# Attention output of a graph-attention layer: 48 mixed matmuls per batch become 64 matmuls of one shape, in another order

## The chip, the cores and the metric

The kernel runs on one NeuronCore of a Trainium2 chip, in one launch. The metric is device time in microseconds (us), measured over whole executions; the kernel before takes 548.71 us (median of 3 runs, 548.39 to 549.91). The engines are named as in the profile: PE is TensorE's matmul side, PEld its weight loads, DVE is VectorE, ACT is ScalarE, POOL is GpSimd, SP issues DMAs.

## The reference

For each of 16 batches there are 512 nodes with 512 features. A dense layer gives `self_feat`; in each of two directions d every node attends, with 16 heads, over the first 20 nodes only. Cut to what matters here:

```python
kv = self_feat[:, :20]
aff = einsum('bnhd,bmhd->bnhm', qh, kh) / sqrt(32)
aff = where(cond > 0, aff, NEG) + label_bias          # per node and key
w = softmax(aff, axis=-1)                             # 512 nodes x 16 heads x 20 keys
out_t = einsum('bnhm,bmf->bnhf', w, kv)
out = einsum('bnhf,hgf->bnhg', out_t, Wout) + bout    # 32 outputs g per head
output = self_feat + out(d=0) + out(d=1)
result = v + relu(output)
```

All of it is in 32-bit floats. The kernel folds `Wout` into the values beforehand, so that per batch the last product is: weights (512 nodes x 640, that is 16 heads x 2 directions x 20 keys) times a block-diagonal value matrix (640 keys x 512 outputs).

## The kernel before, in words

A setup part (up to about 90 us) computes key, bias and value matrices for all batches and writes them to DRAM. Then a loop runs over the batches. Its order is written out by hand: under a manual schedule every engine gets its instructions in the order of the program text. The body for batch b mixes, on PE, the seven score products of batch b (a Strassen-like scheme of seven products in place of eight; helper `score_terms`, line 397, tiles `ps_a`, `ps_c`, `ps_d`), the seven products of the dense layer of batch b+1 (`self_product`, line 667, tile `ps_f`), and near its end the attention output of batch b-1 (`attend`, line 569, tiles `ps_o_f`, `ps_o_c`, and `ps_o_s` at the end of the program). The softmax of a block runs on DVE and ACT (`weigh`, `expo`, `total`), its scaling on POOL (`normal`), and `turn` (line 545) transposes it on DVE in 32x32 blocks into the tile `wt`. The last batch is written out after the loop, with `attend` called for pieces of the nodes.

In `attend`, the weights lie in `wt` with 32 keys on 32 partitions, four such blocks of rows (a = 0 to 3, one per quarter of the nodes), and in the free dimension the key half c (0 or 1), and inside it node groups and five blocks j of 32 keys. The values `vd` lie on the same 32 rows, eight blocks `at` of 32 outputs per key half. Block `at` uses the keys of block j, and it is added to the 32 output partitions `at // 2` of bank a. So `at` = 0, 1 go to output block 0, 2, 3 to block 1, 4, 5 to block 2 and 6, 7 to block 3. `at` 0, 3, 4, 7 are called outer here, 1, 2, 5, 6 inner; 1 and 2 share j = 1, and 5 and 6 share j = 3, so each of these pairs can be one matmul with 64 output columns on two neighbouring output blocks. All matmuls of `attend` add to what `seed_out` (line 556, on ACT) has put into the four PSUM banks before, and `finish` (line 586, on DVE) reads them a loop body later.

A matmul of `attend` uses 32 rows of the PE array (rows of block a) and 32 or 64 columns. Sixteen blocks of 32 by 32 fill the array; so do eight of 32 by 64.

Of the kernel before, what the change touches and what calls it, by code (L numbers as in the profile page):

```python
# [18 lines left out]
def gat_kernel(  # L19
# [21 lines left out]
    B, F, N = xT.shape  # L41
    NG, L = adj.shape[3], adj.shape[4]
    H, DH = 16, 32
# [8 lines left out]
    R = P // HL  # L52
# [41 lines left out]
    ksums, fsums, terms, weighs, smalls, cqD, nzD, outsum, outt, whole = [{} for _ in range(10)]  # L94
# [465 lines left out]
    def attend(b, spans=((0, 0, 2 * HL), (1, 0, 2 * HL)), banks=range(HL)):  # L560


        vd = vds[b].rearrange("p c e i g -> p c (e i g)")
        pairs, ones = ((1, 2, 1), (5, 2, 3)), ((0, 1, 0), (3, 1, 2), (4, 1, 2), (7, 1, 4))
        runs = (ones, spans[:1]), (pairs, spans), (ones, spans[1:])
        for c, lo, hi, at, n, j in [(*span, *of) for group, those in runs for span in those for of in group]:
            for a in banks:
                r = bass.ts(a, R)
                nc.tensor.matmul(  # L569
                    outsum[b][a][bass.ds(at // 2 * DH, n * DH), bass.ds(c * N // 2 + lo * R, (hi - lo) * R)].rearrange(  # L570
                        "p (n r) -> p n r", r=R
                    ),
                    vd[r, c, bass.ds(at * DH, n * DH)],
                    wts[b][r, c].rearrange("p l (g w) -> p (l g) w", g=HL)[:, lo:hi, bass.ts(j, 32)],
                    start=False, stop=n == 1 + (c == 0), skip_group_check=True,
                )

    def spread_out(t, a):
# [120 lines left out]
    with tc.tile_pool(name="setup", bufs=1) as sp, tc.tile_pool(name="ps_acc", bufs=4, space=PSUM) as acc["pool"]:  # L699
# [11 lines left out]
        ones = sp.tile([P, P], F32, name="ones")  # L711
# [6 lines left out]
        with tc.tile_pool(name="setup_k", bufs=1) as sk:  # L718
# [124 lines left out]
            of = {(d, 0): early[:, d] for d in range(2)}  # L843
# [16 lines left out]
        with tc.tile_pool(name="setup_g", bufs=3) as sg:  # L860
# [123 lines left out]
            while units:  # L984
                runs = []
# [84 lines left out]
    with tc.manual_schedule():  # L1070
# [4 lines left out]
        for b in range(B - 1):  # L1075
# [183 lines left out]
            if one:  # L1259
                attend(b - 1)  # L1260
                at(further, feat_sum, b + 1, 2)
                normal(b, 1, 0)
# [19 lines left out]
        b = B - 1  # L1282
# [34 lines left out]
        seed_out(o, 3)  # L1317
        seed_block(b, 1, 1, [accs.tile([P, 2, N // 2], F32, tag=f"f{i}", name=f"ps_e{i}") for i in range(2)])
        attend(o)
        turn(b, 0, 0)  # L1320
        total(b, 1, 0)
# [27 lines left out]
        weigh_plain(b, 1, 1, 1)  # L1349
        turn_part(b, 1, 1, 0)  # L1350
        attend(b, ((0, 0, 8),))
        attend(b, ((1, 0, 4),), range(2))
        spare = const.tile([P, C, WD], F32, tag="g", name=f"o{b}", bufs=1).rearrange("p c w -> p (c w)")
# [66 lines left out]
```

## Time and profile before

| what | value |
|---|---|
| time of whole executions | 548.71 us (548.39 to 549.91) |
| span of the profiled execution | 547.1 us |
| what lies around the span (difference to the median) | 1.6 us |
| PE busy, share of the span | 541.1 us, 99% |
| DVE busy | 481.1 us, 88% |
| POOL, ACT busy | 434 us, 404 us |
| one loop body in the steady part | 28.65 us |
| one `attend` of a whole batch | 2.39 us |
| granted TensorE clock, mean | 0.998 |

How it is read: the span runs from the first to the last instruction of one execution. "Busy" of PE is the union of its matmul records; matmuls are pipelined and the ends of their records are modelled, so what counts below is where records start. Each 32-bit matmul of the program stands in the trace as two passes, each with a weight-load record and a matmul record. The timeline merges neighbouring records of one group into one row with a count (x2); its first column is the start of the first of them in us from the span's start.

### The profile page before, as it was taken

How to read it: one execution, taken by the hardware profiler on the slowest of the kernel's cores; microseconds unless marked ns; L12 is line 12 of the kernel's file. 1: busy time of each engine (PE TensorE's matmuls, PEld its weight loads, DVE VectorE, ACT ScalarE, POOL GpSimd, SP SyncE). 2: the span in 40 equal slices, each digit the busy share in tenths (PEclk: the TensorE clock that was granted, in tenths of full speed). 3: DMA queues.
4: the chain of work that ended last, by engine and by line, in shares of the span. 5: the costliest groups of instructions: out<-in, count | busy, mean ns of one | idle time of the engine just before them, and what ended most of it. 6: DMA issues, size and time to landing. Idle time of an engine off the chain costs nothing.

```text
span 547.1 us, 19673 instructions
## 1 busy us (share of the span) xinstructions
PE 541.1 (99%) x7932; PEld 424.5 (78%) x7932; DVE 481.1 (88%) x711; ACT 404.2 (74%) x999; POOL 433.7 (79%) x418
## 2 busy tenths in 40 slices
PE   9999999999999999999999999999999999999996
PEld 6554368889888878787888888887878788878784
DVE  1776678889999999999999999999999999999996
ACT  1225436798887979888888888887878787978564
POOL 2637996779979797979798888888897979797664
PEclk9999999999999999999999999999999999999999
DMA  8999999978886878788776857676777676736034
GB/s 297 377 394 374 296 367 349 301 228 263 229 257 184 237 218 222 227 221 235 206 232 182 245 182 227 201 231 193 226 209 214 199 227 185 243 91 202 2 116 156
DMA packets 100546, 126.45 MB, mean 231 GB/s; under 512 B 19608, under 2 KB 68694, under 8 KB 98408
## 3 DMA queue, kind: packets, MB, share of 16 engines
q1 hardware_dynamic: 98856, 122.19, 71.7%
q0 software_dynamic: 1168, 2.23, 1.7%
q8 instruction: 62, 1.02, 0.7%
q10 hardware_dynamic: 432, 0.79, 0.4%
q14 instruction: 28, 0.23, 0.2%
HBM read 86.23 MB, written 40.24 MB: 231 GB/s over the span
## 4 chain that ended last, share of the span: by engine, by line
PE 97%; DVE 2%; ACT 0%; issue 0%; DVEq 0%
PE ps_f L667 32%; PE ps_a L397 24%; PE ps_c L397 11%; PE ps_d L397 6%; PE ps_o_f L569 5%; PE ps_v L893 3%; PE ps_k L831 3%; PE ps_kv L781 2%; PE ps_a L284 1%; PE ps_o_c L569 1%; PE ps_l L397 1%; PE ps_c L284 1%; PE ps_warm L737 1%; PE ps_o_s L569 0%; DVE o L611 0%; DVE w L465 0%
## 5 line engine op out<-in xcount | busy, mean ns | idle before, releaser
L327 ACT ACTIVATE prod<-adj,wb_sb 128x80 f32<-128x80 int32 x330 | 116.0, 429 | 0.0
L537 POOL TENSOR_TENSOR w<-w,sm 128x640 f32<-128x640 f32 x63 | 80.2, 1273 | 33.1 <-DVE sm L533 29.5
L667 PE MATMUL ps_f<-t,ws_s 128*64 128x246 f32 x720 | 80.0, 370 | 0.0
L667 PEld LDWEIGHTS ps_f<-t,ws_s 128*64 128x64 f32 x720 | 51.7, 137 | 18.9
L528 ACT ACTIVATE w<-w 128x640 f32<-128x640 f32 x60 | 43.8, 731 | 17.8 <-DVE w L524 17.8
L545 DVE STREAM_TRANSPOSE wt<-w 128x640 f32<-128x640 f32 x63 | 52.4, 833 | 0.1
L667 PE MATMUL ps_f<-x,ws_v 128*64 128x246 f32 x480 | 52.4, 371 | 0.0
L532 DVE TENSOR_REDUCE sm<-w 128x32 f32<-128x640 f32 x63 | 51.1, 811 | 1.1 <-ACT w L528 0.9
L523 DVE TENSOR_REDUCE ps_d<-w 128x32 f32<-128x640 f32 x59 | 48.7, 826 | 1.8 <-ACT ps_d L431 0.2
L524 DVE TENSOR_TENSOR w<-w,ps_d 128x640 f32<-128x640 f32 x59 | 48.4, 820 | 2.0
L667 PEld LDWEIGHTS ps_f<-x,ws_v 128*64 128x64 f32 x480 | 34.7, 137 | 13.0
L370 POOL TENSOR_TENSOR k<-g,k 128x608 f32<-128x608 f32 x30 | 44.7, 1489 | 0.0
L397 PEld LDWEIGHTS ps_a<-g,sf 128*64 128x64 f32 x544 | 34.3, 137 | 5.9 <-issue 5.8
L397 PE MATMUL ps_a<-g,sf 128*64 128x152 f32 x544 | 38.6, 295 | 0.0
L397 PE MATMUL ps_d<-g,sf 128*64 128x152 f32 x544 | 37.9, 293 | 0.0
L338 DVE TENSOR_REDUCE add<-prod 128x80 f32<-128x960 f32 x32 | 36.7, 1146 | 1.1 <-POOL prod L333 1.1
L346 ACT COPY both<-add 64x80 f32<-64x80 f32 x128 | 32.6, 255 | 5.7 <-DVE add L338 4.6
L569 PE MATMUL ps_o_c<-wt,vd 32*32 32x256 f32 (+1 forms) x720 | 36.8, 386 | 0.0
L682 POOL TENSOR_TENSOR t<-x,t 128x492 f32<-128x492 f32 x30 | 34.8, 1161 | 1.2
L397 PEld LDWEIGHTS ps_d<-g,sf 128*64 128x64 f32 x544 | 35.3, 137 | 0.2 <-ACT sf L685 0.2
L333 POOL TENSOR_SCALAR prod<-cond 128x80 f32<-128x80 f32 x32 | 18.0, 563 | 21.8 <-DVE cond L332 20.3
L569 PE MATMUL ps_o_f<-wt,vd 32*32 32x256 f32 (+1 forms) x672 | 34.5, 386 | 0.0
(300 smaller groups left out, 1435.9 us busy)
## 6 DMA issues: line engine op xcount, KB each, us to landing
g<-g_d SPq DMA_DIRECT2D x60, 304.0 KB
g_d<-st SPq DMA_DIRECT2D x16, 1064.0 KB
out_T<-o SPq DMA_DIRECT2D x64, 256.0 KB
x<-in_xT SPq DMA_DIRECT2D x56, 256.0 KB
xn<-in_xn SPq DMA_DIRECT2D x48, 256.0 KB
adj<-in_adj SPq DMA_DIRECT2D x52, 220.0 KB
vd<-bd_d SPq DMA_DIRECT2D x64, 64.0 KB
nz<-nz_d SPq DMA_DIRECT2D x14, 256.0 KB
```

The lines of the kernel that those rows point to most:

```text
L327: nc.scalar.activation(p[:, :, l], a[:, :, l], AF.Identity, scale=wb_sb[:, l : l + 1])
L338: done["masks"] = nc.vector.tensor_reduce(add, prods.pop((b, h)), AX.X, ALU.add)
L370: done["ksum"] = engine.tensor_sub(to, one, two)
L397: nc.tensor.matmul(slot(g)[bass.ts(p, P // 2), : HL * S].rearrange("p (h m) -> p h m", m=NG)[:, :, 1:], of(k)[:, bass.ds(first + g * P // ...
L523: nc.vector.tensor_reduce(mx, f, AX.X, ALU.max)
L524: done["weigh"] = (engine or nc.vector).tensor_sub(f, f, mx.unsqueeze(2).to_broadcast([P, per, NG]))
L528: done["exp"] = nc.scalar.activation(t, t, AF.Exp)
L532: nc.vector.tensor_reduce(sm, heads(weighs[b, c, l]), AX.X, ALU.add)
L537: done["normal"] = nc.gpsimd.tensor_mul(f, f, smalls.pop((b, c, l)).unsqueeze(2).to_broadcast([P, per, NG]))
L545: done["turn"] = nc.vector.transpose(wts[b][:, c, l], weighs.pop((b, c, l)).rearrange("p g w -> p (g w)"))
L569: nc.tensor.matmul(outsum[b][a][bass.ds(at // 2 * DH, n * DH), bass.ds(c * N // 2 + lo * R, (hi - lo) * R)].rearrange("p (n r) -> p n r", ...
L667: nc.tensor.matmul(parts[b][n in (2, 3, 5)][bass.ts(a, P // 2), bass.ts(i, HN)], lhs, x[:, k], start=False, stop=k == 1, skip_group_check= ...
```

## The change

`attend` no longer joins the inner pairs. All matmuls take 32 rows and 32 outputs, and the order is: the outer blocks of key half 0, the outer blocks of key half 1, the inner blocks of key half 0, the inner blocks of key half 1. Before it was: the outer blocks of half 0 (16 matmuls of 32x32), the joined inner pairs of both halves (16 matmuls of 32x64), the outer blocks of half 1 (16 of 32x32). The flag that ends a group is set on the inner blocks. The products and sums are the same. A call for a piece of the nodes goes through the same order with one key half.

```diff
         vd = vds[b].rearrange("p c e i g -> p c (e i g)")
-        pairs, ones = ((1, 2, 1), (5, 2, 3)), ((0, 1, 0), (3, 1, 2), (4, 1, 2), (7, 1, 4))
-        runs = (ones, spans[:1]), (pairs, spans), (ones, spans[1:])
-        for c, lo, hi, at, n, j in [(*span, *of) for group, those in runs for span in those for of in group]:
+        outer, inner = ((0, 0), (3, 2), (4, 2), (7, 4)), ((1, 1), (2, 1), (5, 3), (6, 3))
+        for c, lo, hi, at, j in [(*span, *of) for group in (outer, inner) for span in spans for of in group]:
             for a in banks:
                 r = bass.ts(a, R)
                 nc.tensor.matmul(
-                    outsum[b][a][bass.ds(at // 2 * DH, n * DH), bass.ds(c * N // 2 + lo * R, (hi - lo) * R)].rearrange(
+                    outsum[b][a][bass.ts(at // 2, DH), bass.ds(c * N // 2 + lo * R, (hi - lo) * R)].rearrange(
                         "p (n r) -> p n r", r=R
                     ),
-                    vd[r, c, bass.ds(at * DH, n * DH)],
+                    vd[r, c, bass.ts(at, DH)],
                     wts[b][r, c].rearrange("p l (g w) -> p (l g) w", g=HL)[:, lo:hi, bass.ts(j, 32)],
-                    start=False, stop=n == 1 + (c == 0), skip_group_check=True,
+                    start=False, stop=at in (1, 2, 5, 6), skip_group_check=True,
                 )
```

On PE, in the `attend` of a batch in the steady part, the place where the first 16 matmuls end and the joined pairs begin, before (a row is one matmul, x2 two; 32x256 is 32 outputs by 256 nodes; numbers behind names count buffers):

```order
L569 MATMUL ps_o_f_4208<-wt_3669,vd_4016 32x256
L569 MATMUL ps_o_f_4209<-wt_3669,vd_4016 32x256
L569 MATMUL ps_o_c<-wt_3669,vd_4016 32x256 x2
L569 MATMUL ps_o_f_4208<-wt_3669,vd_4016 64x256
L569 MATMUL ps_o_f_4209<-wt_3669,vd_4016 64x256
L569 MATMUL ps_o_c<-wt_3669,vd_4016 64x256 x2
```

In the changed kernel every row of `attend` is of 32x256, sixteen times these three rows, up to the score products that follow:

```order
L568 MATMUL ps_o_f_4304<-wt_3749,vd_4112 32x256
L568 MATMUL ps_o_f_4305<-wt_3749,vd_4112 32x256
L568 MATMUL ps_o_c<-wt_3749,vd_4112 32x256 x2
L397 MATMUL ps_a_4424<-g_4031,sf_4095 64x8x19 x16
L397 MATMUL ps_d_4426<-g_4031,sf_4095 64x8x19 x16
```

The shape no longer changes inside `attend`, 16 matmuls came in, and what stands before and behind it on PE is the same.

The second place is the end of the program on PE, the pieces of the last batch. Before:

```order
L569 MATMUL ps_o_s_7384<-wt_7357,vd_7251 32x128 x8
L569 MATMUL ps_o_s_7384<-wt_7357,vd_7251 64x128 x4
L569 MATMUL ps_o_s_7398<-wt_7357,vd_7251 32x192 x8
L569 MATMUL ps_o_s_7398<-wt_7357,vd_7251 64x192 x4
L569 MATMUL ps_o_s_7384<-wt_7357,vd_7251 32x64 x8
L569 MATMUL ps_o_s_7384<-wt_7357,vd_7251 64x64 x4
```

And now:

```order
L568 MATMUL ps_o_s_7624<-wt_7597,vd_7475 32x256 x2
L568 MATMUL ps_o_s_7638<-wt_7597,vd_7475 32x256 x2
L568 MATMUL ps_o_s_7624<-wt_7597,vd_7475 32x128 x16
L568 MATMUL ps_o_s_7638<-wt_7597,vd_7475 32x192 x16
L568 MATMUL ps_o_s_7624<-wt_7597,vd_7475 32x64 x18
```

Each piece is one run of equal matmuls in place of two runs of different shape. On the other engines nothing moves.

## The prediction

> **What bounds the kernel now.** I read the page first, then busy times by stretch, then PE's timeline inside one `attend`, since the diff touches nothing else. From the page:
>
> ```profile
> span 547.1 us, 19673 instructions
> PE 541.1 (99%) x7932; PEld 424.5 (78%) x7932; DVE 481.1 (88%) x711; ACT 404.2 (74%) x999; POOL 433.7 (79%) x418
> PEclk9999999999999999999999999999999999999999
> PE 97%; DVE 2%; ACT 0%; issue 0%; DVEq 0%
> q8 instruction: 62, 1.02, 0.7%
> ```
>
> The chain that ended last is PE for 97% of the span, at full clock. Busy times by stretch, cut at the first matmul of two `attend`s and at the first one behind each (columns: stretch, length, busy and records of PE, PEld, DVE, ACT, POOL, clock, DMA share, GB/s):
>
> ```profile
> 286.72:289.12 2.40, 2.40 (x99) 1.19 (x97) 2.28 (x3) 1.34 (x4) 2.32 (x3) 1.00 0.45 127
> 289.12:315.37 26.25, 26.25 (x347) 22.43 (x337) 24.68 (x36) 22.91 (x59) 21.95 (x21) 1.00 0.74 220
> 315.37:317.76 2.39, 2.39 (x98) 1.18 (x96) 2.27 (x3) 1.34 (x4) 2.31 (x3) 1.00 0.39 114
> 317.76:344.01 26.25, 26.25 (x347) 22.43 (x336) 24.69 (x36) 22.93 (x59) 21.94 (x21) 1.00 0.74 219
> ```
>
> PE has no idle time; a body of the loop is 26.25 + 2.39 = 28.65 us, the same each time. So a change of `attend`'s 2.39 us goes into the time one for one, as often as it runs in such a stretch. How often, from the list of the line's instructions (name, records, shortest/median/longest in ns, first and last start):
>
> ```profile
> L569 PE MATMUL ps_o_f<-wt,vd x672: 373/375/425, 143.3 to 518.0; 32*32 32x256 f32 x112, 32*64 32x256 f32 x56
> ```
>
> Two of four banks, 12 matmuls each, two passes each: 48 records per `attend`, so 672 are 14 of them, all in the stretch that PE bounds. The fifteenth (530.84) and the pieces of batch 15 lie in the tail, below.
>
> **The change part by part.** Inside one `attend` (PE's timeline; each row two records, `ps_o_f` banks 0 and 1, `ps_o_c` banks 2 and 3):
>
> ```profile
> 315.37 0.41 PE L569 MATMUL ps_o_f<-wt,vd 32*32 32x256 f32 x2
> 315.38 0.41 PE L569 MATMUL ps_o_c<-wt,vd 32*32 32x256 f32 x2
> 315.39 0.40 PE L569 MATMUL ps_o_f<-wt,vd 32*32 32x256 f32 x2
> ...
> 315.61 0.38 PE L569 MATMUL ps_o_f<-wt,vd 32*32 32x256 f32 x2
> ...
> 315.70 0.38 PE L569 MATMUL ps_o_c<-wt,vd 32*32 32x256 f32 x2
> 316.01 0.43 PE L569 MATMUL ps_o_f<-wt,vd 32*64 32x256 f32 x2
> 316.03 0.44 PE L569 MATMUL ps_o_c<-wt,vd 32*64 32x256 f32 x2
> 316.07 0.44 PE L569 MATMUL ps_o_f<-wt,vd 32*64 32x256 f32 x2
> 316.10 0.44 PE L569 MATMUL ps_o_c<-wt,vd 32*64 32x256 f32 x2
> 316.28 0.38 PE L569 MATMUL ps_o_f<-wt,vd 32*64 32x256 f32 x2
> ...
> 316.50 0.38 PE L569 MATMUL ps_o_f<-wt,vd 32*64 32x256 f32 x2
> ...
> 316.71 0.38 PE L569 MATMUL ps_o_f<-wt,vd 32*64 32x256 f32 x2
> ...
> 317.12 0.41 PE L569 MATMUL ps_o_f<-wt,vd 32*32 32x256 f32 x2
> 317.13 0.41 PE L569 MATMUL ps_o_c<-wt,vd 32*32 32x256 f32 x2
> 317.14 0.40 PE L569 MATMUL ps_o_f<-wt,vd 32*32 32x256 f32 x2
> ```
>
> Three groups, A (outer, half 0), B (pairs), C (outer, half 1): 0.64 + 1.11 + 0.64 us. In A the first passes of all 16 matmuls start within 0.1 us (eight rows, 0.013 apart, 6.7 ns per matmul), and the second passes from 315.61 on: a block of the array takes its second pass when its first has streamed, and other blocks' matmuls run past it meanwhile. B has eight blocks, so four rounds.
>
> *What is removed: two changes of shape.* Inside B a round follows the last by 0.215 us (316.28, 316.50, 316.71). The last round before another shape takes 0.40 (315.61 to 316.01, 316.71 to 317.12), the first one 0.24 to 0.27. The change keeps eight rounds (64 matmuls, 16 at a time, two passes) and one shape: if rounds simply followed each other, 0.24 + 6 x 0.215 + 0.40 = 1.93 us, 0.46 less than now.
>
> [...]
>
> *What is added: groups that follow each other without a pause, each of 16 x 4 = 64 instructions* (two weight loads and two matmuls per matmul). Whether PE has them at hand in time is not shown for one shape, but A to B shows how supply works. B's first matmuls start at 316.01, but the rows then come 0.033 apart, 16.7 ns per matmul, where A's and C's come 6.7 ns apart. The blocks they need were free, so their instructions were late: 4.2 ns each. Counting back, matmul 3 (316.03) is the ninth to twelfth instruction of B, so delivery restarted at about 316.03 - 0.03 - 8 x 0.004 = 315.97. What happened there is that A's oldest second pass ended: 315.61 + 0.375 = 315.98. Reading: PE holds a fixed number of instructions, a place is given back in program order only when its matmul has ended, and A's 64 fill it. A itself fits (all 16 start at full pace), so the number is at least 61; B's ninth was no longer in, so it is below 64 + 9 = 73. C is the cross-check: when it starts, half of B is already given back and the rest follows at once, and C's rows come at 0.013.
>
> [...]
>
> In the changed kernel A, C and the two inner groups are such groups of 64. From a group's start: the oldest second pass starts at 0.24, ends at 0.24 + 0.375 = 0.615, and the next group's second matmul starts 0.03 later, at 0.65 (the first, whose leading three instructions fit in, at 0.46), then one per 16.7 ns, though its blocks were free from 0.46 on. So groups follow each other by 0.65 us, not by 2 x 0.215 = 0.43: starts 0, 0.65, 1.30, 1.95. In the fourth the last matmul comes some 12 steps of 16.7 ns later (2.15), its second pass 0.24 after that (2.39), and the next work 0.31 behind (315.70 to 316.01): **2.70 us, against 2.39, +0.31**.
>
> Bounds: below, 1.93 us (supply never late); above, supply restarts only when the whole group has ended, 0.24 + 0.10 + 0.375 + 0.03 = 0.745 per group, 3 x 0.745 + 0.15 + 0.64 = 3.03 us (+0.64). I take 2.70, since it is the reading that fits both A to B and B to C. Fourteen times: **+4.3 us** (-6.4 to +9.0).
>
> *More instructions to fetch.* The 15,864 PE instructions are 62 packets (1.02 MB); about 16 x 16 x 4 more add four packets. Now 192 instructions pass in 2.39 us without a stall; then 256 in 2.70, 95 against 80 per us. I take 0; if one late packet cost 0.1 us at every `attend`, it would be 1.4.
>
> *The tail.* Its chain of waits, in order of time:
>
> ```profile
> 526.78 4.16 PE ps_l L397 x64
> 530.93 0.02 issue
> 530.96 0.83 DVE mx L463
> ...
> 535.59 0.48 DVE mx L463
> ...
> 538.89 0.27 ACT w L468
> ...
> 539.90 2.38 PE ps_o_s L569 x85
> 542.28 0.02 issue
> 542.31 0.42 DVE o L611
> ```
>
> From 530.96 to 538.87 the chain is DVE, so the fifteenth `attend`'s +0.31 lies beside it, unless it makes the scores late that DVE takes at 535.59; then up to +0.3. From 539.90 PE is on the chain, in small pieces with five changes of shape inside them: about -0.4 if all of that went, but the last piece waits for a transpose that DVE ends near 541.25 and is itself two groups of 64. I take 0 (-0.4 to +0.3).
>
> Sum: profiled execution 547.1 + 4.3 = 551.4 us of span; with 1.6 around it, on the median 548.7, **553.0 us**. Waits elsewhere do not grow: PE gets later, all others keep their order.
>
> **The rivals.**
>
> *Faster: supply keeps up.* 14 x -0.46 = -6.4, tail -0.3: 542.0. [...] Against: B's late rows need another cause; B's wider weight loads (64 columns) could be one. It decides if places are given back at a matmul's start rather than its end. DVE would have to follow:
>
> ```profile
> 305.00 0.82 DVE L509 TENSOR_TENSOR w<-ps_c,w 128x640 f32<-128x640 f32 x1 [0.77 <-POOL w L500]
> 315.49 0.82 DVE L503 TENSOR_TENSOR w<-ps_a,both 128x640 f32<-128x640 f32 x1 [0.28 <-PE ps_a L397]
> ```
>
> Its waits in a body, 0.77 and 0.28, both hang on PE's scores and shrink with them, so 1.05 covers 0.46.
>
> *Slower by less: each group costs what A costs now.* 4 x 0.64 = 2.58 us, +0.19, 14 times +2.6: 551.3. This is so if refilled instructions come at 6.7 ns. Against: B's 16.7 ns.
>
> *No change:* gain and loss cancel, 548.7, if places return about halfway, near 0.4 us after the start of a group. Nothing in the rows asks for it.
>
> *Slower by more:* supply restarts after a whole group, or fetching stalls: up to 557.7. Against: B's restart came with A's oldest matmul, 0.09 before its last.
>
> That the change does not do what it says is ruled out by the order of the instructions.
>
> **How the numbers follow.** Forecast 553.0: 0.64. Slower by less 0.12, slower by more 0.05, no change 0.05, supply keeps up 0.14. The likeliest one's own range is 551.8 to 554.5 (0.22 to 0.41 us per `attend`). A range of 549.0 to 555.5 leaves out the faster case and the far end of the slow one. A measurement of this kernel can tell 0.3% (1.6 us) from no change: faster 0.14, same 0.06, slower 0.80.
>
> **What would show it.** Right: `attend` takes about 2.70 us, the body 28.95; the second group's first row stands near +0.46, its others from +0.65 at 0.033 apart, with 0.1 to 0.2 us gaps between rounds; no change of DVE's or ACT's waits except longer ones on PE. Wrong: rows of `attend` in eight rounds 0.215 apart and a body of 28.2 us (then places are given back early), or a body of 28.65 with waits of PE on another engine.

## The result, and the profile after

The changed kernel takes 555.22 us (median of 4 executions, 554.18 to 556.47), the kernel before 548.73 us (4 executions, 548.39 to 549.91). The ratio is 1.0113, with a 95% interval of 1.0094 to 1.0132: **6.2 us slower** by the ratio, 6.5 us by the two medians, where +4.3 us was forecast (553.0 us). The median lies inside the stated range of 549.0 to 555.5 us, 0.3 us below its upper end; two of the four executions lie above it. The direction and the mechanism held; the forecast ratio of 1.0078 lies below the interval, so some 2 us came from somewhere else.

One correction to the words on the kernel before: the row block `a` is a pair of head groups and half of the nodes, and `c` picks the head group inside the pair. Nothing in the argument rests on it.

The rows of the page of the changed kernel that answer to those of before (its execution took 554.77 us):

```profile
span 552.9 us, 20745 instructions
PE 546.3 (99%) x8468; PEld 444.2 (80%) x8468; DVE 480.9 (87%) x711; ACT 404.9 (73%) x999; POOL 433.8 (78%) x418
PEclk9999999999999999999999999999999999999998
PE 98%; DVE 1%; issue 0%; POOL 0%; DVEq 0%; POOLq 0%
q8 instruction: 66, 1.08, 0.8%
```

PE is still the chain, at full clock (0.997); it has 536 matmul records more, and the instruction queue brought four packets more, as counted beforehand. Now three bodies of the loop, each cut into its `attend` and the rest (columns as before: stretch, length, busy and records of PE, PEld, DVE, ACT, POOL, clock, DMA share, GB/s):

```profile
259.19:261.88 2.69, 2.69 (x129) 1.81 (x128) 2.57 (x3) 1.62 (x5) 2.61 (x3) 1.00 0.56 144
261.88:288.13 26.25, 26.25 (x342) 22.42 (x336) 24.36 (x36) 22.64 (x58) 21.65 (x21) 1.00 0.82 215
288.13:291.51 3.38, 3.21 (x130) 1.84 (x128) 3.21 (x4) 2.04 (x6) 3.30 (x4) 1.00 0.59 167
291.51:317.76 26.25, 26.25 (x345) 22.43 (x336) 23.73 (x35) 22.33 (x56) 20.96 (x20) 1.00 0.72 219
317.76:320.45 2.69, 2.69 (x130) 1.81 (x128) 2.56 (x3) 1.63 (x5) 2.61 (x3) 1.00 0.37 100
320.45:347.09 26.64, 26.59 (x342) 26.10 (x336) 24.37 (x36) 22.77 (x58) 21.66 (x21) 1.00 0.75 205
```

The first is the plain case: `attend` takes 2.69 us (2.70 forecast) and the rest 26.25 us as before, so a body is 28.94 us (28.95 forecast). The second `attend` takes 3.38 us at the same clock, and PE is idle for 0.17 us inside it. In the third the `attend` is plain, but the rest takes 26.64 us. Before, all bodies from the second on were 28.65 us. So there are two effects: +0.29 us in every body, and something irregular.

A plain `attend` on PE's timeline (each row two records or so; the first two rows and the last of a group, and the first ones of the next):

```profile
317.78 0.41 PE L568 MATMUL ps_o_f<-wt,vd 32*32 32x256 f32 x2
317.79 0.41 PE L568 MATMUL ps_o_c<-wt,vd 32*32 32x256 f32 x2
...
317.87 0.41 PE L568 MATMUL ps_o_c<-wt,vd 32*32 32x256 f32 x2
318.02 0.38 PE L568 MATMUL ps_o_f<-wt,vd 32*32 32x256 f32 x2
...
318.23 0.59 PE L568 MATMUL ps_o_f<-wt,vd 32*32 32x256 f32 x2
318.44 0.40 PE L568 MATMUL ps_o_c<-wt,vd 32*32 32x256 f32 x1
...
318.48 0.41 PE L568 MATMUL ps_o_f<-wt,vd 32*32 32x256 f32 x2
318.51 0.41 PE L568 MATMUL ps_o_c<-wt,vd 32*32 32x256 f32 x2
...
319.08 0.41 PE L568 MATMUL ps_o_c<-wt,vd 32*32 32x256 f32 x2
...
319.72 0.40 PE L568 MATMUL ps_o_c<-wt,vd 32*32 32x256 f32 x1
...
320.14 0.39 PE L568 MATMUL ps_o_c<-wt,vd 32*32 32x256 f32 x2
320.47 0.35 PE L397 MATMUL ps_a<-g,sf 128*64 128x152 f32 x2
```

From the start at 317.78: the first group's 16 matmuls start at full pace (0.09 us), their second passes from +0.24. The second group's first matmul stands at +0.46 (the row of 318.23 joins it to a pass of the first group), its others from +0.65 (318.44), about 0.033 apart per pair. The third group begins at +1.30, the fourth at +1.95; the last pass stands at +2.39, the next work at +2.69. Forecast were 0.46, 0.65, 1.30, 1.95, 2.39 and 2.70.

**Where the 5.9 us between the two profiled executions went** (spans of 547.06 and 552.93 us; starts of the first matmul of an `attend` in the two traces):

| stretch | before | after | difference |
|---|---|---|---|
| start of the program to the first `attend` | 143.26 | 142.47 | -0.79 |
| first to fourteenth `attend` (13 bodies) | 372.63 | 378.59 | +5.96 |
| from the fourteenth to the end | 31.17 | 31.87 | +0.70 |

The first row lies ahead of the changed code. Of the second, 13 x (28.940 - 28.647) = 3.81 us is the regular part; **2.15 us is irregular**. The bodies of the changed kernel from the second to the thirteenth take, in order, 28.94, 29.05, 29.16, 28.94, 29.63, 29.33, 28.94, 28.94, 29.13, 28.94, 29.07 and 28.94 us, which is 1.73 us over the plain time; the other 0.42 us lies in the first body, which also stops, at 147.36. The third row is +0.29 for the fourteenth `attend` and +0.41 behind it.

What stands at the irregular places: PE's timeline in the `attend` of 3.38 us:

```profile
290.35 0.39 PE L568 MATMUL ps_o_f<-wt,vd 32*32 32x256 f32 x2
290.38 0.37 PE L568 MATMUL ps_o_c<-wt,vd 32*32 32x256 f32 x1
290.93 0.37 PE L568 MATMUL ps_o_c<-wt,vd 32*32 32x256 f32 x1 [0.17 <-issue]
290.93 0.41 PE L568 MATMUL ps_o_f<-wt,vd 32*32 32x256 f32 x2
```

PE waits for nothing that the profile shows ("issue"). All PE instructions (matmuls, weight loads and semaphore instructions) counted in order from the program's start, 193 modulo 256 stand before the stop. A packet of the instruction queue holds 16.4 KB (1.08 MB in 66 packets). That this is 256 PE instructions is an estimate from the counts: the 16,936 matmul and weight-load records come to 257 for each packet, the 15,864 of before in 62 packets to 256, and with the semaphore instructions the 17,160 here to 260. With 64 instructions held, an estimate too (the rows of before allow 61 to 72), PE's intake was then at a packet's end, 193 + 64 = 257. The nearest packet of the instruction queue began at 288.64 and ended at 289.63, 1.3 us before work went on. The other irregular places (at 147.36, 203.44, 234.51, 322.41, 409.41 and 465.24) stand at about the same count, 190 to 219 modulo 256, each 2.3 to 3.2 us behind the start of a packet. That is a pattern, not yet a proof; the experiments below test it. In four of the bodies another 0.06 to 0.12 us (0.43 us in all) comes at the body's end. The last of the busy times above shows the state in which these bodies run after a stop: weight loads are busy for 26.10 us in place of 22.4. The score products end in a plain body with two records that start together (317.549 and 317.555); in this one they end with a single one, 0.13 us behind the last two (346.755 and 346.759, then 346.888). Read so, their two column halves stand one pass apart after a stop, and the pass is paid at the end; this reading was not tested.

### The profile page after: what moved, and what is told of

It is laid out like the page before. It is cut to its first block, busy times and chain, and to the rows that moved or that the text cites. A ratio compares the mean times of both kernels' runs of the same rounds, so it can differ in the third digit from the quotient of the medians.

```text
span 552.9 us, 20745 instructions
## 1 busy us (share of the span) xinstructions
PE 546.3 (99%) x8468; PEld 444.2 (80%) x8468; DVE 480.9 (87%) x711; ACT 404.9 (73%) x999; POOL 433.8 (78%) x418
## 3 DMA queue, kind: packets, MB, share of 16 engines
q8 instruction: 66, 1.08, 0.8%
## 4 chain that ended last, share of the span: by engine, by line
PE 98%; DVE 1%; issue 0%; POOL 0%; DVEq 0%; POOLq 0%
PE ps_f L666 32%; PE ps_a L397 24%; PE ps_c L397 11%; PE ps_d L397 6%; PE ps_o_f L568 4%; PE ps_v L892 3%; PE ps_o_c L568 3%; PE ps_k L830 3%; PE ps_kv L780 2%; PE ps_a L284 1%; PE ps_l L397 1%; PE ps_c L284 1%; PE ps_warm L736 1%; PE ps_e L397 0%; PE ps_o_s L568 0%; PE ps_d L284 0%
## 5 line engine op out<-in xcount | busy, mean ns | idle before, releaser
L666 PE MATMUL ps_f<-t,ws_s 128*64 128x246 f32 x720 | 81.2, 370 | 0.0
L666 PEld LDWEIGHTS ps_f<-t,ws_s 128*64 128x64 f32 x720 | 56.3, 136 | 15.5
L666 PEld LDWEIGHTS ps_f<-x,ws_v 128*64 128x64 f32 x480 | 37.6, 137 | 10.6
L568 PE MATMUL ps_o_c<-wt,vd 32*32 32x256 f32 x960 | 41.9, 385 | 0.2 <-issue 0.2
L397 PE MATMUL ps_a<-g,sf 128*64 128x152 f32 x544 | 39.8, 296 | 0.1
L568 PE MATMUL ps_o_f<-wt,vd 32*32 32x256 f32 x896 | 39.2, 385 | 0.0
L496 ACT ACTIVATE w<-ps_a 128x640 f32<-128x640 f32 x30 | 21.1, 703 | 19.2 <-PE ps_a L397 19.0
```

The costliest lines, as they stand in the source:

```text
L397: nc.tensor.matmul(slot(g)[bass.ts(p, P // 2), : HL * S].rearrange("p (h m) -> p h m", m=NG)[:, :, 1:], of(k)[:, bass.ds(first + g * P // ...
L568: nc.tensor.matmul(outsum[b][a][bass.ts(at // 2, DH), bass.ds(c * N // 2 + lo * R, (hi - lo) * R)].rearrange("p (n r) -> p n r", r=R), vd[ ...
L666: nc.tensor.matmul(parts[b][n in (2, 3, 5)][bass.ts(a, P // 2), bass.ts(i, HN)], lhs, x[:, k], start=False, stop=k == 1, skip_group_check= ...
```

## The experiments

Theory **W** (for window): PE holds about 64 instructions (61 to 72 by the rows of before) and gives a place back in program order, when its matmul has ended. Theory **S**: supply is no limit, and a change of shape or something in the wide weight loads made the rows late. A drain, in the words of S, is no more than a measured difference: before, the last round ahead of another shape took 0.40 us, and a round inside the pairs 0.215. **F**: the irregular part is instruction packets that come late. The kernels were each profiled in one execution; the first was also timed against the kernel before.

### Two groups of one shape, then the pairs

The kernel before, with one of its two changes of shape taken away and its 48 matmuls kept:

```diff
-        runs = (ones, spans[:1]), (pairs, spans), (ones, spans[1:])
+        runs = (ones, spans), (pairs, spans)
...
-                    start=False, stop=n == 1 + (c == 0), skip_group_check=True,
+                    start=False, stop=n == 2, skip_group_check=True,
```

> The kernel before with its 48 matmuls, the 32 of 32x32 of both halves put ahead of the 16 joined pairs: one change of shape fewer, and two groups of 64 instructions of one shape in a row. Theory W (PE holds about 64 instructions and gives a place back in program order when its matmul has ended): the second group starts 0.65 us behind the first, not 0.43; one attend takes 1.43 + 1.10 = about 2.5 us against 2.39 before; time +1 to +2 us, 549.7 to 550.7. Rival S (only the array's rounds of 0.215 us and the drains at a change of shape count): 0.24 + 3 x 0.215 + 0.40 = 1.29 less 0.22 for the drain that is gone, so 2.17 us per attend and 545.5. Theory F (the changed kernel's few longer loop bodies are late instruction packets, since 256 instructions pass in 2.7 us): 192 instructions per attend as before, so all loop bodies are equally long.

Measured: 550.15 us (10 executions) against 549.57 us (13), ratio 1.0016 (1.0006 to 1.0026), so 0.3 to 1.4 us slower; W had named +1 to +2, and 14 times the 0.08 us found below is 1.1. Busy times of one body, cut into the two narrow groups, the pairs, and the rest:

```profile
287.71:289.13 1.42, 1.42 (x66) 0.81 (x64) 1.29 (x2) 0.73 (x2) 1.34 (x2) 1.00 0.66 175
289.13:290.18 1.05, 1.05 (x37) 0.59 (x32) 1.05 (x2) 0.69 (x3) 1.05 (x2) 1.00 0.42 146
290.18:316.43 26.25, 26.25 (x344) 22.42 (x336) 24.59 (x36) 22.85 (x59) 21.88 (x21) 1.00 0.76 218
```

`attend` takes 2.47 us: a change of shape is gone, and it is 0.08 us longer than the 2.39 of before. Its timeline shows the second narrow group late, as in the changed kernel, and the pairs behind it on time:

```profile
288.38 0.40 PE L569 MATMUL ps_o_c<-wt,vd 32*32 32x256 f32 x1
...
288.45 0.41 PE L569 MATMUL ps_o_c<-wt,vd 32*32 32x256 f32 x2
288.48 0.41 PE L569 MATMUL ps_o_f<-wt,vd 32*32 32x256 f32 x2
...
289.14 0.43 PE L569 MATMUL ps_o_f<-wt,vd 32*64 32x256 f32 x2
289.16 0.43 PE L569 MATMUL ps_o_c<-wt,vd 32*64 32x256 f32 x2
289.17 0.43 PE L569 MATMUL ps_o_f<-wt,vd 32*64 32x256 f32 x2
```

The narrow rows come 0.033 apart, 0.66 us behind the first group (287.72); the pairs' rows come 0.013 apart. In the kernel before it was the pairs whose rows were 0.033 apart. So the lateness does not belong to the wide loads: it belongs to whatever comes behind a full group without a pause. S falls; W had named the interval (0.65 us) and the `attend` (about 2.5 us). All bodies from the second on are 28.73 us, so here is no irregular part: 192 instructions in 2.47 us.

### Half the array's rows

The changed kernel, whose whole-batch `attend` runs only two of the four row blocks; half of the attention output of those batches is left out. A round then has 8 matmuls, 32 instructions, so that the next round fits beside it:

```diff
+        if len(spans) == 2:
+            banks = range(2)
```

> The changed kernel with a whole batch's attend for banks 0 and 1 alone: banks 2 and 3 keep what the seed put there, so half of the attention output is left out. Groups are of 8 matmuls (32 instructions), so two groups fit into the 64 places. Theory W: the rounds then follow each other by 0.215 us in one shape, eight rounds, attend 0.24 + 6 x 0.215 + 0.40 = 1.9 us; loop body 26.25 + 1.9 = 28.15. Rival G (a group of one shape behind another costs 0.65 us by itself, for instance since it writes the same banks): 4 x 0.65 = 2.6 us, body 28.9. Theory F: 128 instructions per attend, all bodies equally long.

Measured: 542.32 us. Busy times of its `attend` and of the rest of the body:

```profile
312.33:314.22 1.89, 1.89 (x66) 1.13 (x64) 1.76 (x2) 1.01 (x2) 1.81 (x3) 1.00 0.59 158
314.22:340.47 26.25, 26.25 (x344) 22.57 (x336) 24.89 (x37) 23.27 (x60) 22.48 (x21) 1.00 0.78 217
```

It is the same chain of eight rounds on every block of the array in use, in the same order and of one shape, and it takes 1.89 us in place of 2.69. That is the time which the rival "supply keeps up" had worked out for all four banks (1.93 us). So rounds of one shape can follow each other at 0.215 us. W's reading is that four banks' instructions don't come fast enough. This run alone would also fit a limit that appears only with all 16 blocks at work; the next one keeps them all at work and changes the length of a stream.

### Shorter streams, twice the matmuls

The changed kernel with each half of the nodes in its own matmuls: 128 matmuls of 128 nodes, with the same columns streamed in all.

```diff
-    def attend(b, spans=((0, 0, 2 * HL), (1, 0, 2 * HL)), banks=range(HL)):
+    def attend(b, spans=((0, 0, HL), (0, HL, 2 * HL), (1, 0, HL), (1, HL, 2 * HL)), banks=range(HL)):
```

> The changed kernel with each matmul of a whole batch's attend split into two of 128 nodes: 128 matmuls, the same sums and the same array time. Theory W: eight groups of 64 instructions; a group's oldest second pass starts at 0.03 + 0.107 = 0.135 us and ends 0.27 later, so groups follow by about 0.43 us: 7 x 0.43 + 0.25 + 0.4 = 3.4 to 3.6 us per attend, body at least 29.7. Rival S: array time is unchanged, 1.95 us, body 28.2. Theory F: 512 instructions in 3.5 us is a faster demand than in the changed kernel, so nearly every attend shows stalls on top (0.3 us or more each), and the bodies differ in length.

Measured: 606.09 us. Its timeline:

```profile
307.61 0.30 PE L568 MATMUL ps_o_f<-wt,vd 32*32 32x128 f32 x2
...
308.06 0.30 PE L568 MATMUL ps_o_c<-wt,vd 32*32 32x128 f32 x2
...
310.63 0.27 PE L568 MATMUL ps_o_c<-wt,vd 32*32 32x128 f32 x1
312.66 0.27 PE L568 MATMUL ps_o_c<-wt,vd 32*32 32x128 f32 x1 [1.76 <-issue]
```

Groups of 16 start at 0, 0.43, 0.86, 1.30, 1.73, 2.16, 2.60 and 3.03 us: 0.433 apart where it was 0.65. So the interval follows the length of a stream, as it does where a place comes back at a matmul's end, and not a fixed refill time alone. Eight groups at this pace are 3.46 us. The rest is the row with 1.76 us of "issue": work stops for 2.02 us (310.63 to 312.66). From the first `attend` on, the loop has 19 stops of 0.7 to 3.2 us, in every body at least one, and before each of them the count of PE instructions is 193 modulo 256. The `attend`s of this kernel take 5.15 to 7.63 us, its bodies 31.4 to 36.5 us. This speaks for F: 512 instructions in 3.5 us were more than the queue brought.

### By output block

The changed kernel, its 64 matmuls sorted by output block, so that each run of 16 uses a quarter of the array's columns and works in a chain of its own:

```diff
-        for c, lo, hi, at, j in [(*span, *of) for group in (outer, inner) for span in spans for of in group]:
+        order = [(*span, *of) for group in (outer, inner) for span in spans for of in group]
+        for c, lo, hi, at, j in sorted(order, key=lambda of: of[3] // 2):
```

> The changed kernel with the same 64 matmuls sorted by output block: all four matmuls of output block 0 for each bank, then block 1, 2, 3. Sixteen matmuls in a row then use 4 of the 16 blocks of the array. Theory W: no more than about 16 matmuls are in flight, so at most the blocks of one or two output blocks work at a time; the next output block starts 0.65 us behind the last, and its matmul k not before the last one's matmul k has ended: 3 x 0.65 + 8 x 0.215 + 0.5 = 4.1 to 4.6 us per attend, body 30.4 to 30.9. Rival S (blocks run independently, matmuls pass each other without limit): 1.95 us, body 28.2; a rival in which only the second matmul on the same block and bank is slow: 2.7 us, body 28.95.

Measured: 585.08 us; `attend` takes 4.79 us in each body, and all bodies from the second on are 31.05 us.

```profile
298.10 0.41 PE L569 MATMUL ps_o_f<-wt,vd 32*32 32x256 f32 x2
...
298.34 0.38 PE L569 MATMUL ps_o_f<-wt,vd 32*32 32x256 f32 x2
...
298.99 0.38 PE L569 MATMUL ps_o_f<-wt,vd 32*32 32x256 f32 x2
...
299.01 0.40 PE L569 MATMUL ps_o_f<-wt,vd 32*32 32x256 f32 x2
...
302.89 0.35 PE L397 MATMUL ps_a<-g,sf 128*64 128x152 f32 x2
```

With three quarters of the array idle at its start, PE doesn't reach the second output block's matmuls until 299.01, 0.91 us in, although nothing but their place in the order holds them. That speaks against S, and against a cost of the second matmul on the same block alone, which would have been 2.7 us. It bears W out in direction, not in size (4.1 to 4.6 us per `attend`): by W the second block was due at about 0.65, and its leading instructions earlier still, since in the changed kernel the first matmul of the second group starts at +0.46. The weight loads (PEld) there:

```profile
298.99 0.11 PEld L569 LDWEIGHTS ps_o_f<-wt,vd 32*32 32x32 f32 x2
299.00 0.11 PEld L569 LDWEIGHTS ps_o_c<-wt,vd 32*32 32x32 f32 x2
299.01 0.11 PEld L569 LDWEIGHTS ps_o_f<-wt,vd 32*32 32x32 f32 x2
```

The first block has eight rounds of loads, four matmuls in a row of two passes each. The second block's first loads (299.01) come right behind the sixth round (298.99), and the last two rounds follow at 299.20 and 299.42. So something holds the second block until most of the first block's loads are out, without strict program order among the loads; what it is stays open. The kernel has the same 256 instructions per `attend`, spread over 4.79 us in place of 2.69, and no irregular body: here a stop came with the rate at which a packet is used up, not with the number of packets.

### The same kernel, its packets shifted

The changed kernel with 84 PE instructions more at the start of the program; the loop is untouched, but every packet ends 84 instructions earlier in it:

```diff
+            for _ in range(21):
+                nc.tensor.matmul(warm[:, :4], ones, ones[:, :4], start=True, stop=True)
```

> The changed kernel with 21 more tiny matmuls (128x4) among those that warm PE up at the start; nothing else is changed. They are 84 PE instructions, a third of a packet of 256, so in the loop every packet of instructions ends 84 instructions earlier than in the changed kernel. Counted from the start of the program, the instruction number at the starts of the attends, modulo 256, goes through about 142, 57, 228 in turn in the changed kernel (a body has 939 = 3 x 256 + 171), and the bodies that are longer than 28.94 us are those of 142 and 228, never those of 57. F (the longer bodies come from late packets of instructions): the numbers become about 226, 141, 56 in turn, so the shortest bodies are now the third, sixth, ninth and twelfth (28.94 us), the first, fourth, seventh and tenth lose time inside the attend (0.1 to 0.7 us) and the second, fifth, eighth and eleventh about 4 us behind its start (0.1 to 0.4 us). The total stays about the same, 554 to 556 us. Rival D (they come from data transfers or another engine at these places of the program): the second, fifth, eighth and eleventh bodies stay at 28.94 us, and the third, sixth and twelfth stay longer.

Measured: 562.34 us, against 548.06 us for the kernel before, one execution each; 554 to 556 us was expected. It starts its loop 7.3 us later than the changed kernel, since the added matmuls (their records start at 4.0 to 9.7 us) delay the setup, and so only the bodies count. They take, from the second to the thirteenth, 28.94 us, except the seventh (29.36) and the tenth (29.37). The sixth, of 29.63 us in the changed kernel, and the seventh, now the longer one, in busy times:

```profile
294.64:297.33 2.69, 2.69 (x130) 1.81 (x128) 2.56 (x3) 1.63 (x5) 2.61 (x3) 1.00 0.45 138
297.33:323.58 26.25, 26.25 (x341) 22.44 (x336) 24.39 (x36) 22.64 (x58) 21.67 (x21) 1.00 0.75 216
323.58:326.69 3.11, 3.11 (x130) 1.84 (x128) 2.95 (x4) 2.03 (x6) 3.03 (x4) 1.00 0.46 125
326.69:352.93 26.24, 26.24 (x344) 22.43 (x336) 23.98 (x35) 22.32 (x56) 21.23 (x20) 1.00 0.74 214
```

The sixth is plain. The two longer bodies are among the four for which F had named a loss inside the `attend`, at a count of 228 and 229 at its start, and the loss stands at 189 to 219 modulo 256 again, as in the changed kernel. The third, sixth, ninth and twelfth are all plain, as F had it, and rival D (data transfers or another engine at these places of the program) falls: the third, sixth and twelfth should have stayed longer. F missed in part: of eight bodies that were to be longer only these two are. The first and the fourth, named for a loss inside the `attend` too, lost nothing, and neither did those with a count of 141 to 144, which were to lose 0.1 to 0.4 us behind it. So the count says where a loss can be; whether it comes must depend on something else, presumably on when the packet arrives. In the last batch of this kernel it came too. From its chain of waits:

```profile
552.82 0.70 issue
553.52 0.51 PE ps_o_s L568 x28
```

The restart at 553.52 is at 193 modulo 256, and the last packet ahead of it had begun at 551.18. In the changed kernel the same place of the count lies at 547.58, where its chain has the smaller gap:

```profile
547.46 0.12 issue
547.58 0.56 PE ps_o_s L568 x24
```

None of the kernels that compute the whole output beats the kernel before. In its order, with the pairs between two narrow groups, the late rows of the pairs are the only sign of the window; whether another order would do better was not tried.

## Why the prediction was right or wrong, point by point

- **What bounds the kernel**: right. The plain bodies carry the difference one for one, 26.25 us beside `attend` in both kernels.
- **What is removed: two changes of shape**: right as a part, and not enough. The trace of before has 0.40 us for a round ahead of another shape against 0.215 inside the pairs, and 1.89 us with half the rows shows that rounds of one shape do follow each other. But the run with one change of shape fewer was 0.08 us per `attend` slower, so no run shows a change of shape as a cost by itself.
- **What is added: places given back in program order at a matmul's end**: right, to 0.01 us at every point of the timeline, and in three other orders: 0.433 us between groups with half the stream, 2.47 us with two groups in a row, 1.89 us with half the instructions per round. The fourth, by output block, was 0.2 us above the top of what was expected, and its second block came later than this rule gives. The term "+4.3 us" measured 14 x 0.293 = 4.1 us.
- **"More instructions to fetch. I take 0"**: this is the term that was mis-sized. It measured 2.15 us over the 13 bodies, in the one profiled execution. The prediction had an alternative of the same kind (0.1 us at every `attend`, 1.4 us) and dismissed it because 192 instructions in 2.39 us went without a stop. That took a case without stops for the kernel's own: 192 in 2.39 us or in 2.47 us and 256 in 4.79 us cost nothing, 256 in 2.69 us costs 0.1 to 0.7 us in seven of the 13 bodies, and 512 in 3.5 us cost 1.7 to 6.8 us in each.
- **The tail, 0 (-0.4 to +0.3)**: it measured +0.41, above its bound of +0.3; the gap of 0.12 us at 547.46 is part of it, at the same place of the count.
- **The sum**: 4.1 + 2.15 + 0.41 = 6.7 us, less 0.79 us ahead of the loop, is the 5.9 us between the profiled executions (6.2 us by the ratio of the executions, 6.5 us by their medians). Whether that 0.79 is more than chance is open.
- **The range**: the likeliest case's own range, 0.22 to 0.41 us per `attend`, holds the 0.29 us that a plain one takes more, but its 551.8 to 554.5 us misses the time. That 555.22 still lies within 549.0 to 555.5 is in part luck: stops in fetching were taken as 0 in the sum, and the 0.79 us gained ahead of the loop helped.
- **"Waits elsewhere do not grow"**: right for what bounds the kernel: DVE is busy for 480.9 us against 481.1, and PE waits for no other engine in the loop. Waits of the others did grow with PE's delay (DVE on `ps_d` in the loop, 0.4 to 6.8 us), as the signs named for it allowed, and cost nothing.
- **The rivals**: "supply keeps up" needed 1.93 us per `attend`, which came only with half the instructions. "Each group costs what A costs now" needed 2.58. "Slower by more" had two causes; a restart after a whole group is ruled out by the 0.65 us between groups, and the stall in fetching is what came, beside the 4.1 us and at less than that case's full price.

## What to carry to other kernels

Where many small matmuls run side by side on blocks of the PE array, count instructions in flight and not only blocks: here a group of 16 32-bit matmuls (64 instructions, two rounds) came 0.65 us behind the one before it, where rounds with half the instructions followed each other at about 0.215 us; one long run of equal small matmuls (2.69 us) was slower than shorter runs with the pairs, at half the instructions per output, between them (2.39 us). In this kernel a wide matmul that does two blocks' work was worth more than the two changes of shape that came with it, by 0.29 us an `attend`. And a claim that "instruction fetch has room" needs the local rate in the densest 256 instructions (an `attend` of 2.69 us here), not the mean of the kernel.

## What the runs showed of the hardware that was not expected

PE's instructions came in packets of 16.4 KB (1.08 MB in 66), by their counts about 256 each, and PE stopped at the same count modulo 256 where they were used up fast (190 to 219 in the changed kernel, 193 at all 19 stops with the shorter streams): with 256 in 2.69 us seven of 13 bodies lost 0.1 to 0.7 us, with 512 in 3.5 us every body lost 1.7 to 6.8 us, and with 192 in 2.39 us or 256 in 4.79 us none lost any. Why a stop lasts until 1.3 to 1.8 us after the packet's record has ended (seven places of the changed kernel), and why one packet is late and another at the same count is not, stays open: no run here varied the other transfers.
